# Where the expert values of a two-layer kernel are put down: by slot or by token

## The chip, the cores and the metric

The kernel runs on one core of a Trainium2 chip. The metric is the device time of one launch in microseconds (us), lower is better. The core has five instruction streams that run side by side and meet at semaphores: PE (matrix multiplication, with PEld for its weight loads), DVE (vector), ACT (scalar), POOL (general purpose) and SP (here only an issuer of DMAs). Plain DMAs are issued by SP; an indirect DMA, whose row addresses come from an index tile, is issued by POOL.

## The reference

Two layers work on x of shape 4 x 1024 x 256 (batch b, position, feature D). Each has an attention part and a mixture of experts. The mixture of layer 0, which the change is about:

```python
logits = einsum('bsd,de->bse', h, Wr) + br            # 8 experts
route_w = softmax(logits); topk 2; renormalised       # two experts per token
hid = relu(einsum('bsd,edh->ebsh', h, W1) + b1)       # 256 -> 1024
expert_out = einsum('ebsh,ehd->ebsd', hid, W2) + b2   # 1024 -> 256
x = x + gb * einsum('bse,ebsd->bsd', routed, expert_out)
```

Layer 1 first normalises this x, runs a gated product with three weights (w0, w2: 256 to 1024, w1: back) over 8 chunks of 128 positions, each chunk scaled by a decay that depends on the loss of the chunks before, and then has a second, smaller mixture (8 experts of 256 x 256, two per token). All is float32.

## The kernel before, in words

**Tokens, pairs, blocks, slots.** There are 4096 tokens in 32 tiles of 128 (tile c*4+b is chunk c of batch b). Each token has two pairs (token, expert). Only the chosen experts are computed: the pairs are sorted by expert into blocks of 128 slots, a block has one expert, and there can be up to J = 71 blocks (2*32+8-1). 68 of them are always worked through (`passed` = J - SPARE); the last 3 only in a branch that is taken if the data need them.

**Prologue** (to about 115 us). Layer 0's attention part, normalisation and router. The normalised rows go to the DRAM tensor `h_rows` (`store`, L1231), one row per token and one row of ones for empty slots. `route` (L376) marks each token's two experts; `close_staged` (L544) lays out the blocks; `limits` and `list_weights` (L675) give the tables from which the later steps work.

**Blocks** (to about 640 us). For each block j: `reach`, `look`, `find` compute which 128 tokens it holds (three blocks ahead); `fetch` gathers their rows of `h_rows` into one of four buffers `xgbuf` (two blocks ahead); `turn_rows` and `rows_turned` transpose them on PE and copy them to `xT`; `weights_in` and `weights_out` gather W1 and W2 of its expert into one of two buffers each, where a table entry out of bounds makes the gather skip weights that are there already; `hidden` (PE, p_h) and `rectified` (ACT) give the hidden rows; `values` (PE, p_y) and `biased` (DVE) the 128 values; `kept` (L1625) stores them to rows j*128 and following of the DRAM tensor `y0`. The first 60 blocks (`turning` = J - LATE) are a loop written out by hand, in which p_y runs one block behind p_h. The order in it on POOL is `weights_in(j + 1)`, `weights_out(j)`, `fetch(j + 2)`. Small steps of the side work (`once`, L1650) are strewn into it: ranks of pairs within their expert (`ranks`, `places`), routing weights, and from them `slot`, the row of `y0` at which each pair's values lie (`weights`, L751, a generator of which one step runs per block).

**The last blocks and the combination.** Blocks 60 to 67 (`late_block`, `late_values`) are pieces of a planner, `Plan`: each piece has an engine, an estimated duration, predecessors, buffers that it holds and a rank; the planner simulates the engines and writes the instructions out in the order in which it started the pieces, and that order is then fixed on each engine. Among these pieces is the combination of the first two chunks: layout and block order are such that the first 8 tiles (FIRST) have all their pairs in the first 60 blocks. `combine` (L1408) does a tile: two gathers from `y0` by `slot` into a buffer `yg` of 128 x 2 x 256 (three buffers), ACT scales the first by its routing weight, DVE adds the second, multiplies by the gate and adds to x.

**Layer 1.** A second plan holds everything after: the combination of the other six chunks, then for every chunk normalisation (`normal`), the gated product (`fast`: p_u, p_f) and layer 1's mixture, whose pairs are in two groups `ga` and `gb`, with their own gathers from `ga_y` and `gb_y`.

Every gather goes through one helper, L330, so in the profile the tiles tell them apart: `w<-in_W,g_wrow`, `xg<-h_rows,g_row`, `yg<-y,g_slot`.

Of the kernel before, what the change touches and what calls it, by code (L numbers as in the profile page):

```python
# [19 lines left out]
P = 128  # L20
# [3 lines left out]
E = 8  # L24
# [9 lines left out]
AHEAD = 3  # L34
W1ROW = KD * H + KH
# [102 lines left out]
def adaln_d2_kernel(  # L138
# [95 lines left out]
    xgbuf = [pw.tile([P, D], F32, name=f"xg_{i}") for i in range(4)]  # L234
# [34 lines left out]
    lane = iota("lane", [[0, 1]], [P, 1], mult=1)  # L269
    count = iota("count", [[1, P]], [P, P])  # L270
# [71 lines left out]
    class Pairs:  # L342
# [4 lines left out]
        def __init__(self, pool, scratch, name, n):  # L347
            def t(shape, dt, what, of=pool):
                return of.tile(shape, dt, name=f"{name}_{what}", bufs=1)

            self.n, self.J, self.name = n, blocks_of(n), name

            self.part = min(n, P // E)
            self.halves = n // self.part
            self.K = self.part * E
            self.one = t([P, 2, n, E], F16, "one")
            self.best = t([P, 2, n], F32, "best")
            self.w = t([P, 2, n], F32, "w")
            self.pos = t([P, 2, n], F32, "pos")
            self.slot = t([P, 2, n], I32, "slot")  # L360
            self.row = t([P, self.J], I32, "row")
            self.wrow = t([P, self.J], I32, "wrow")
            self.start = t([P, E], F32, "start")


            self.more = t([P, self.halves, P + 1], F16, "more")
            nc.vector.memset(self.more[:, :, P : P + 1], 1.0)
            self.limit = t([P, self.halves, self.J], F32, "limit")
            self.nth = t([P, self.J], F32, "nth")

            self.both = t([P, n + 1, E], F16, "both")
            nc.vector.memset(self.both[:, 0, :], 0.0)
            self.pairs = t([P, self.halves, P], F16, "pairs")
            self.base = t([P, self.halves], F32, "base", scratch)

        def route(self, scratch, logits, bias, at, k, step=1):  # L376
# [14 lines left out]
            for i in range(2):  # L391
# [10 lines left out]
                first = scratch.tile([P, k], F32, tag=f"r{k}_first", name="r_first", bufs=2)  # L402
# [272 lines left out]
        def list_weights(self, scratch):  # L675
# [18 lines left out]
            )  # L694

# [54 lines left out]

        def weights(self, scratch):  # L751

            n, up1, origin = self.n, self.up1, self.origin

            def t(shape, what, dt=F32):
                return scratch.tile(shape, dt, tag=f"g_{what}", name=f"g_{what}", bufs=1)


            d = t([P, n], "d")
            nc.vector.tensor_tensor(d, self.best[:, 0, :], self.best[:, 1, :], ALU.subtract)  # L760
            nc.scalar.activation(d, d, AF.Tanh, scale=0.5)
            for i, sign in ((0, 0.5), (1, -0.5)):
                nc.vector.tensor_scalar(self.w[:, i, :], d, sign, 0.5, ALU.mult, ALU.add)
            start = t([P, E], "start1")
            nc.vector.memset(start[:, E - 1 :], 0.0)
            nc.vector.tensor_copy(start[:, : E - 1], origin[:, 1:E])
            own = t([P, E], "own_n")
            nc.vector.tensor_tensor(own, up1[:, 1:], up1[:, :E], ALU.subtract)
            jump = t([P, E], "jump")
            nc.vector.tensor_tensor(jump, origin[:, E:], start, ALU.subtract)  # L770
            one = self.one.rearrange("p i n e -> p (i n) e")
            of = []
            for what, by in (("at", start), ("own", own), ("jump", jump)):
                yield
                mine = t([P, 2 * n, E], "mine")
                nc.vector.tensor_tensor(
                    mine, one, by.unsqueeze(1).to_broadcast([P, 2 * n, E]), ALU.mult
                )
                yield
                r = t([P, 2 * n], f"of_{what}")  # L780
                nc.vector.tensor_reduce(r, mine, AX.X, ALU.add)
                of.append(r)
            yield
            at, own, jump = of
            pos = self.pos.rearrange("p i n -> p (i n)")

            nc.vector.scalar_tensor_tensor(own, own, float(P), pos, ALU.mult, ALU.is_lt)
            nc.vector.tensor_tensor(own, own, jump, ALU.mult)
            nc.vector.tensor_tensor(at, at, own, ALU.add)
            nc.vector.tensor_scalar(at, at, float(P), -1.0, ALU.mult, ALU.add)  # L790
            nc.vector.tensor_tensor(
                self.slot.rearrange("p i n -> p (i n)"), at, pos, ALU.add
            )
# [25 lines left out]


# [14 lines left out]
    h_rows = dram.tile([B * S + 1, D], F32, name="h_rows")  # L835
    for k in range(KD):
        nc.sync.dma_start(h_rows[B * S :, k * P : (k + 1) * P], ones[:1, :])
    sT0 = silu_of(0, c0)
# [305 lines left out]
    def second_half(b):  # L1144
# [64 lines left out]
        for gs in routed:  # L1209
# [14 lines left out]
            for g in gs:  # L1224
                of_batch["route", b, g] = d
            for g in gs:
                back, slot, key = backs[g]

                def store(g=g, key=key):
                    at = 4 * g * B * P  # L1230
                    nc.sync.dma_start(  # L1231
                        h_rows[at : at + 4 * B * P, :].rearrange(
# [135 lines left out]
    y0 = dram.tile([g0.J * P, D], F32, name="y0")  # L1368
    for j in range(g0.J - SPARE, g0.J):
        for k in range(KD):  # L1370
            nc.sync.dma_start(y0[j * P : (j + 1) * P, k * P : (k + 1) * P], ones)
# [36 lines left out]
    def combine(key, c, kind, y, g, tile_of, bias, gate, after, rank, at=0.0):  # L1408

        done = []  # L1410
        for b in range(B):
# [3 lines left out]
            for i in range(2):  # L1415

                def fetch(b=b, s=s, i=i):
                    if i == 0:
# [3 lines left out]
                got.append(  # L1422
                    plan(
                        POOL, 1.28, fetch, after=after, holds=[slot], rank=rank, at=at, lag=1.5
                    )
                )

# [196 lines left out]
    def kept(j, y):  # L1624
        return plain(nc.sync.dma_start(y0[j * P : (j + 1) * P, :], y))  # L1625
# [22 lines left out]
    steps = g0.weights(work)  # L1648

    def once(j):  # L1650

        if j == 3:
            g0.places(work, g0.ranks(ps_m))
# [4 lines left out]
        if j >= 6:  # L1658
            next(steps, None)
# [3 lines left out]
    with tc.manual_schedule(engines=ORDERED | {EngineType.SP}):  # L1663
        for j in range(2):
            g0.fetch(xgbuf[j], h_rows, j)
        xT, hid = rows_turned(turn_rows(0)), None
        for j in range(turning):

            weights_in(j + 1)
            if j:  # L1670
                weights_out(j)
# [6 lines left out]
            xT = rows_turned(turn_rows(j + 1))  # L1678
            g0.find(work, g0.look(ps_m, reached), j + AHEAD)
            if j:  # L1680
                kept(j - 1, biased(j - 1, values(j - 1, hid)))
# [7 lines left out]
    def late_block(j):  # L1689
# [65 lines left out]
        def turned_():  # L1755
            made[key, "xT"] = rows_turned(made[key, "pt"])

        if j > turning:
            t = plan(PE, 0.27, turn, after=of_block.get(("rows", j), []), holds=[ps], rank=at - 0.6)
            d = plan(DVE, 0.45, turned_, after=[t], holds=[ps, xTs], rank=at - 0.6)  # L1760
# [19 lines left out]
    def late_values(j, hids, after):  # L1780
# [7 lines left out]
        def out_():  # L1788
            made[key, "y"] = biased(j, made[key, "p2"])

        if j == passed - 1:
# [4 lines left out]
            SP, 0.1, lambda: kept(j, made[key, "y"]), after=[d], holds=[ys], rank=at, lag=2.2  # L1796
# [3 lines left out]
    made[("b", turning - 1), "hid"] = hid  # L1800

# [26 lines left out]
    for c in range(FIRST // B):  # L1828
# [4 lines left out]
            y0[: turning * P, :],  # L1833
# [4 lines left out]
            [of_block["kept", turning - 1]],  # L1838
            50.0 + c,
        )  # L1840
# [7 lines left out]
    with tc.If(filled > passed, preferred_fallthrough_block=True, label="late"):  # L1848
# [3 lines left out]
        for j in range(passed, g0.J):  # L1852
# [6 lines left out]
            kept(j, biased(j, values(j, hid)))  # L1859
# [444 lines left out]
    for c in range(NC):  # L2304
# [3 lines left out]
        else:  # L2308
# [4 lines left out]
                y0,  # L2313
# [132 lines left out]
```

## Time and profile before

| | |
|---|---|
| time, median of 3 runs | 1153.02 us (1152.88 to 1153.03) |
| the profiled execution, its own time | 1154.62 us |
| its span, first to last instruction | 1152.6 us |
| mean granted clock of PE | 0.987 |
| busy: PE, DVE, ACT, POOL | 1100.8, 586.6, 425.1, 410.6 us |
| POOL's indirect DMAs: weights w, rows xg, values yg of layer 0 | 134, 68, 64 |
| their mean time on POOL | 998, 966, 959 ns for w, xg, yg |
| stores of y by SP | 68, of 128 KB each |

The profile is of one execution. Its busy times are sums over the span; a line such as `2.80 <-DVE xT L1572` in brackets says that the engine sat idle for 2.80 us before the instruction and that DVE's writing of `xT` at line 1572 ended it. [...] Starts and lengths of PE's matmuls are as issued; they are pipelined.

### The profile page before, as it was taken

The numbers are of one execution on the slowest core, as the hardware profiler recorded it, in microseconds if no ns is written. First come the engines' busy times: TensorE is split into PE (matmuls) and PEld (weight loads), VectorE is DVE, ScalarE is ACT, GpSimd is POOL, SyncE is SP. The second block draws the span as 40 slices with busy tenths as digits, with TensorE's granted clock in tenths as the row PEclk, the third lists the DMA queues.
The fourth block names the chain that finished last, engine by engine and source line by source line (L and its number), as shares of the span: only waits on it lengthen the run. The fifth ranks groups of instructions, "written<-read, shape, count | busy, mean of one in ns | idle before, by whom it ended". The sixth has DMA issues, their size and how long they took to land. (4 is left out here: it accounts for less than half of the span.)

```text
span 1152.6 us, 18406 instructions
## 1 busy us (share of the span) xinstructions
PE 1100.8 (96%) x6236; PEld 872.3 (76%) x6236; DVE 586.6 (51%) x2245; ACT 425.1 (37%) x1148; POOL 410.6 (36%) x477
## 2 busy tenths in 40 slices
PE   8999999999999999999989989999999999999893
PEld 5996899999999999999978455675667676646751
DVE  7777233222222212222245589878587535787566
ACT  5975333233333323233324433423324325342421
POOL 1000444333443344333463452420124332644644
PEclk8999999999999999999998999999999999999997
DMA  9412514564522415151251211200013323342544
GB/s 320 163 54 92 178 50 147 192 220 151 188 78 75 156 33 193 37 188 38 74 197 46 66 55 52 62 29 18 1 38 104 112 71 97 102 127 86 147 108 130
DMA packets 79369, 123.18 MB, mean 107 GB/s; under 512 B 23646, under 2 KB 63076, under 8 KB 74668
## 3 DMA queue, kind: packets, MB, share of 16 engines
q0 software_dynamic: 31680, 69.61, 19.9%
q1 hardware_dynamic: 46492, 50.80, 13.3%
q10 hardware_dynamic: 1104, 1.58, 0.4%
q8 instruction: 52, 0.85, 0.3%
q14 instruction: 41, 0.34, 0.1%
HBM read 205.18 MB, written 30.58 MB: 205 GB/s over the span
## 5 line engine op out<-in xcount | busy, mean ns | idle before, releaser
L1599 ACT ACTIVATE hid<-p_h,w 128x128 f32<-128x128 f32 x544 | 155.1, 368 | 338.0 <-issue 257.1
L1587 PEld LDWEIGHTS p_h<-xT,w 128*128 128x128 f32 x2176 | 255.4, 193 | 7.8 <-DVE xT L1572 4.0
L1587 PE MATMUL p_h<-xT,w 128*128 128x128 f32 x2176 | 257.1, 277 | 3.8 <-DVE xT L1572 3.2
L1610 PE MATMUL p_y<-w,hid 128*128 128x256 f32 x1088 | 251.6, 384 | 3.2 <-issue 3.2
L1884 PE MATMUL p_u<-hT,a 128*128 128x512 f32 x512 | 230.7, 595 | 0.8 <-ACTq L1848 0.8
L330 POOL DMA_INDIRECT w<-in_W,g_wrow x134 | 133.7, 998 | 271.6 <-ACT hid L1599 129.9
L1610 PEld LDWEIGHTS p_y<-w,hid 128*128 128x128 f32 x1088 | 202.6, 191 | 29.2 <-issue 4.2
L1884 PEld LDWEIGHTS p_u<-hT,a 128*128 128x128 f32 x512 | 94.2, 190 | 97.2 <-issue 89.3
L1572 DVE COPY xT<-pm_x 128x256 f32<-128x256 f32 x68 | 28.8, 424 | 186.8 <-PE pm_x L1567 176.4
L1932 PE MATMUL p_f<-a,hf 128*128 128x256 f32 x512 | 116.8, 380 | 3.9 <-DVE ln_mv L1467 1.6
L1621 DVE TENSOR_TENSOR y<-p_y,w 128x256 f32<-128x256 f32 x68 | 28.8, 424 | 176.1 <-PE p_y L1610 176.1
L1932 PEld LDWEIGHTS p_f<-a,hf 128*128 128x128 f32 x512 | 95.9, 190 | 22.6 <-issue 5.7
L330 POOL DMA_INDIRECT xg<-h_rows,g_row x68 | 65.7, 966 | 123.7 <-DVE g_hits L734 103.3
L330 POOL DMA_INDIRECT yg<-y,g_slot x64 | 61.4, 959 | 86.7 <-DVE x_sb L1444 33.5
L2193 PE MATMUL p_e<-ew,xT 128*128 x280 | 70.4, 384 | 0.3 <-ACT y L2203 0.3
L330 POOL DMA_INDIRECT xg<-ga_rows,ga_row x39 | 37.2, 954 | 91.3 <-DVE ga_row L743 35.0
L1896 ACT ACTIVATE hf<-p_u,decay 128x512 f32<-128x512 f32 x56 | 38.0, 683 | 72.6 <-PE p_u L1884 68.5
L2193 PEld LDWEIGHTS p_e<-ew,xT 128*128 128x128 f32 x280 | 49.4, 190 | 10.6 <-issue 5.1
L1507 DVE TENSOR_TENSOR h<-h,mod 128x256 f32<-128x256 f32 x128 | 51.5, 425 | 9.2 <-ACT h L1497 6.3
L1900 DVE SCALAR_TENSOR_TENSOR hf<-p_u,decay,hf 128x512 f32<-128x512 f32 x56 | 41.9, 748 | 21.8 <-PE p_u L1884 14.5
L2203 ACT COPY y<-p_e 128x256 f32<-128x256 f32 x70 | 26.0, 371 | 57.1 <-PE p_e L2193 24.8
L1980 POOL TENSOR_TENSOR x_sb<-x_sb,step 128x256 f32<-128x256 f32 x32 | 23.7, 743 | 62.2 <-DVE step L1973 44.5
(363 smaller groups left out, 1283.6 us busy)
## 6 DMA issues: line engine op xcount, KB each, us to landing
y<-y SPq DMA_DIRECT2D x68, 128.0 KB
ga_y<-y SPq DMA_DIRECT2D x39, 128.0 KB
x_sb<-in_x SPq DMA_DIRECT2D x8, 512.0 KB
h_rows<-xn SPq DMA_DIRECT2D x8, 512.0 KB
gb_y<-y SPq DMA_DIRECT2D x31, 128.0 KB
out_x<-x_sb SPq DMA_DIRECT2D x7, 512.0 KB
a<-in_fw SPq DMA_DIRECT2D x6, 512.0 KB
mod<-mod_rows SPq DMA_DIRECT2D x6, 512.0 KB
```

Source lines behind the costliest of these rows:

```text
L330: return nc.gpsimd.indirect_dma_start(out=dst, out_offset=None, in_=table, in_offset=bass.IndirectOffsetOnAxis(ap=index, axis=0), bounds_c ...
L1507: nc.vector.tensor_tensor(h, h, mods1[(sc, sh)[i]][:, b, :], (ALU.mult, ALU.add)[i])
L1572: nc.vector.tensor_copy(xT, pt)
L1587: nc.tensor.matmul(p1[:, i, :], lhsT=w1[:, k * H + m * P : k * H + (m + 1) * P], rhs=xT[:, k, :], start=(k == 0), stop=(k == KD - 1),)
L1599: nc.scalar.activation(hid[:, m, :], p1[:, i, :], AF.Relu, bias=w1buf[j % 2][:, KD * H + m : KD * H + m + 1],)
L1610: nc.tensor.matmul(p2, lhsT=hid[:, m, :], rhs=w2[:, m * D : (m + 1) * D], start=(m == 0), stop=(m == KH - 1),)
L1621: nc.vector.tensor_tensor(y, p2, w2buf[j % 2][:, KH * D :], ALU.add)
L1884: nc.tensor.matmul(pu, lhsT=a[:, k, m * P : (m + 1) * P], rhs=made["n1", c, "hT"][:, k, :, :], start=(k == 0), stop=(k == KD - 1),)
L1896: nc.scalar.activation(made[key, m], made[key, m, 0], AF.Silu, scale=decays[c])
L1900: nc.vector.scalar_tensor_tensor(h, made[key, m, 1], decays[c], h, ALU.mult, ALU.mult)
L1932: nc.tensor.matmul(made[key, "p2", b], lhsT=made[key, m][:, b * P : (b + 1) * P], rhs=a1[:, m, :], start=(m == 0), stop=(m == KH - 1),)
L2193: nc.tensor.matmul(made[key, "p2"], lhsT=made[key, "xT"][:, k, :], rhs=ew_flat[:, bass.ds(made[key, "at"] + k * D, D)], start=(k == 0), st ...
```

## The change

Each gathered row now brings with it where its values belong. A row of `h_rows` has two more elements (DX = 258): the code of the token's first expert (8 minus its number) and twice the token's place (row 2*(s*128+p) for token p of tile s). Small plain DMAs (`mark`) write both, eight bytes per token, after each call of `route`; the row of the empty slots gets a number beyond the last row. After a block's rows are transposed, `aim` computes on DVE, for each of its 128 slots, twice the token's place plus 1 if the block's expert is not the token's first. `put` stores the block's values to those rows of `y0` by an indirect DMA on POOL; rows beyond the end are skipped. `y0` now has 2 rows for each of 4096 tokens, and `combine` reads a tile's 128 x 2 x 256 values by one plain load on SP, which waits for the puts that can hold its pairs (the first 60 for the first two chunks, all for the others). In the loop the put of block j - 2 stands between `weights_in(j + 1)` and `weights_out(j)` on POOL. The ranks within an expert, `places` and the computation of `slot` are gone for layer 0, and so are the fills of the three spare blocks of `y0`. Layer 1's mixture keeps its slots and gathers.

The diff, cut to its core:

```diff
+DX = D + 2
-    xgbuf = [pw.tile([P, D], F32, name=f"xg_{i}") for i in range(4)]
+    xgbuf = [pw.tile([P, DX], F32, name=f"xg_{i}") for i in range(4)]
+    twice = iota("twice", [[2 * P, NC * B]], [P, NC * B], mult=2)
...
+            self.meta = t([P, n, 2], F32, "meta")
+            nc.vector.tensor_copy(self.meta[:, :, 1], twice[:, :n])
+            self.beyond = t([P, 2], F32, "beyond")
+            nc.vector.memset(self.beyond, float(2 * n * P))
+            self.code = t([P, self.J], F32, "code")
...
-                first = scratch.tile([P, k], F32, tag=f"r{k}_first", name="r_first", bufs=2)
+                if i == 0:
+                    first = self.meta[:, cut, 0]
+                else:
+                    first = scratch.tile(
+                        [P, k], F32, tag=f"r{k}_first", name="r_first", bufs=2
+                    )
...
+            nc.vector.tensor_scalar(
+                self.code, self.pb[:, 0, :], -1.0, float(E), ALU.mult, ALU.add
+            )
...
+        def aim(self, scratch, xg, j):
+            dest = scratch.tile([P, 1], I32, tag="g_dest", name="g_dest", bufs=8)
+            nc.vector.scalar_tensor_tensor(
+                dest, xg[:, D : D + 1], self.code[:, j : j + 1],
+                xg[:, D + 1 : D + 2], ALU.not_equal, ALU.add,
+            )
+            return dest
+
+        def put(self, table, dest, y):
+            return plain(
+                nc.gpsimd.indirect_dma_start(
+                    out=table,
+                    out_offset=bass.IndirectOffsetOnAxis(ap=dest, axis=0),
+                    in_=y,
+                    in_offset=None,
+                    bounds_check=2 * self.n * P - 1,
+                    oob_is_err=False,
+                )
+            )
...
+    def put(name, *args):
+        ins = groups_of[name].put(values_of[name], *args)
+        for others in (name, f"{name} read"):
+            tc.declare_no_dep(ins, group=others, reason="other places")
+        tc.add_to_no_dep_group(name, ins)
+        puts.setdefault(name, []).append(ins)
...
-    h_rows = dram.tile([B * S + 1, D], F32, name="h_rows")
+    h_rows = dram.tile([B * S + 1, DX], F32, name="h_rows")
+    nc.sync.dma_start(h_rows[B * S :, D:], g0.beyond[:1, :])
...
+            def mark(k=k, at=at):
+                first = at - at % B
+                nc.sync.dma_start(
+                    h_rows[first * P : (first + k * B) * P, D:].rearrange(
+                        "(c b p) d -> b p c d", b=B, p=P
+                    )[at % B],
+                    g0.meta[:, at : at + (k - 1) * B + 1 : B, :],
+                )
+            plan("SP", 1.0, mark, after=[d], rank=rank)
...
-    y0 = dram.tile([g0.J * P, D], F32, name="y0")
-    for j in range(g0.J - SPARE, g0.J):
-        for k in range(KD):
-            nc.sync.dma_start(y0[j * P : (j + 1) * P, k * P : (k + 1) * P], ones)
+    y0 = dram.tile([2 * B * S, D], F32, name="y0")
...
+            def load(b=b, s=s):
+                t = made[key, c, b] = buf(kind, [P, 2, D])
+                y = values_of[g.name][2 * s * P : 2 * (s + 1) * P, :]
+                ins = plain(nc.sync.dma_start(t, y.rearrange("(p i) d -> p i d", i=2)))
+                if stage is not None:
+                    tc.declare_no_dep(
+                        ins, group=g.name, keep=puts[g.name][:stage], reason="other places"
+                    )
+                    tc.add_to_no_dep_group(f"{g.name} read", ins)
+                behind(ins, puts[g.name][:stage])
+            if y is None:
+                f = plan(SP, 0.1, load, after=after, holds=[slot], rank=rank, at=at, lag=2.7)
+                got = [f, f]
...
-        if j == 3:
-            g0.places(work, g0.ranks(ps_m))
-        if j >= 6:
-            next(steps, None)
+        if j == 6:
+            g0.weights(work)
...
             weights_in(j + 1)
+            if j > 1:
+                kept(j - 2)
             if j:
                 weights_out(j)
             g0.fetch(xgbuf[(j + 2) % 4], h_rows, j + 2)
...
             xT = rows_turned(turn_rows(j + 1))
+            aimed(j + 1)
             g0.find(work, g0.look(ps_m, reached), j + AHEAD)
             if j:
-                kept(j - 1, biased(j - 1, values(j - 1, hid)))
+                ys0[j - 1] = biased(j - 1, values(j - 1, hid))
...
         of_block["kept", j] = plan(
-            SP, 0.1, lambda: kept(j, made[key, "y"]), after=[d], holds=[ys], rank=at, lag=2.2
+            POOL, 1.0, lambda: kept(j), after=[d], holds=[ys], rank=at, lag=2.2
         )
+    of_block["kept", turning - 2] = plan(
+        POOL, 1.0, lambda: kept(turning - 2), at=0.4, rank=-2.0, lag=2.2
+    )
...
-            y0[: turning * P, :],
+            None,
...
-            [of_block["kept", turning - 1]],
+            [of_block["kept", turning - 2], of_block["kept", turning - 1]],
             50.0 + c,
+            stage=turning,
```

## The prediction

> **What bounds the kernel now.** I read the page first, then the table of busy time by stretch, then the timeline where PE falls behind. The page, busy time of the engines and PE's row of the 40 slices:
>
> ```profile
> PE 1100.8 (96%) x6236; PEld 872.3 (76%) x6236; DVE 586.6 (51%) x2245; ACT 425.1 (37%) x1148; POOL 410.6 (36%) x477
> ...
> PE   8999999999999999999989989999999999999893
> ```
>
> PE is busy in all but 1152.6 - 1100.8 = 51.8 us. By 20 us stretches, 6.3 of the idle lie before 40 us and 17.6 after 1120; from 140 to 580 there is none. What this change can win is where its reads are: from 575 us, when the first pairs are gathered. The same table, cut at the start of the matmuls p_h of blocks 60 to 67 (the last row ends at layer 1's first p_u); columns: stretch, length, then busy us of PE, PEld, DVE, ACT, POOL, clock, DMA share, GB/s:
>
> ```profile
> 569.19:576.60 7.41, 7.41 (x55) 6.91 (x53) 1.60 (x7) 2.28 (x8) 3.23 (x4) 1.00 0.54 178
> 576.60:586.98 10.38, 7.58 (x55) 6.89 (x53) 3.58 (x12) 3.30 (x10) 6.46 (x7) 1.00 0.86 297
> 586.98:596.08 9.10, 9.10 (x53) 8.60 (x53) 4.80 (x15) 2.79 (x9) 5.81 (x6) 0.81 0.45 135
> 596.08:609.42 13.34, 10.09 (x55) 8.04 (x53) 5.99 (x25) 4.16 (x13) 6.70 (x8) 0.81 0.31 102
> 609.42:617.80 8.38, 8.32 (x52) 7.55 (x51) 5.13 (x16) 2.92 (x10) 5.01 (x6) 0.89 0.31 81
> 617.80:625.15 7.35, 7.35 (x51) 6.94 (x51) 4.83 (x14) 3.35 (x13) 3.93 (x4) 1.00 0.13 38
> 625.15:640.17 15.02, 13.04 (x81) 11.31 (x79) 8.20 (x29) 6.83 (x17) 1.00 (x1) 1.00 0.12 37
> ```
>
> A block takes 7.41 us with the two count matmuls, 7.35 without. Four blocks take 10.38, 9.10, 13.34 and 8.38, part of it at half clock. Why, shows in the timeline (bracket: idle before, and who ended it):
>
> ```profile
> 575.02 0.96 POOL L330 DMA_INDIRECT yg<-y,g_slot  x1 [2.79 <-issue]
> ...
> 580.23 0.38 PE L1567 MATMUL pm_x<-ident,xg 128*128 128x128 f32 x2
> ...
> 583.94 0.94 POOL L330 DMA_INDIRECT yg<-y,g_slot  x1 [0.30 <-issue]
> ...
> 586.50 0.42 DVE L1572 COPY xT<-pm_x 128x256 f32<-128x256 f32 x1 [5.10 <-remote]
> 586.98 5.24 PE L1587 MATMUL p_h<-xT,w 128*128 128x128 f32 x30 [2.80 <-DVE xT L1572]
> ```
>
> PE's transposes pm_x ran at 580.23, yet DVE's copy of them starts at 586.50 and PE then waits for it. The trace's semaphore updates from PE stop at 579.28 and resume at 585.76, seven within 1.0 us. The same happens in each of POOL's long runs of indirect DMAs 0.30 us apart: 8 of them in 575.02 to 584.89, 10 in 591.30 to 603.78, 6 in 608.60 to 615.95, 13 in 646.71 to 662.67, 8 in 667.63 to 677.34. PE's updates stop 3.7 to 7.5 us after the first and come back at 585.76, 605.69, 617.25, 665.20 and 677.58. In the loop, with three such DMAs per block, no silence is longer than 3.6 us; in layer 1 spacings up to 5.2 are normal, so the fifth case is weak. So I read: a long unbroken run on POOL holds back PE's signals, and whoever waits for PE stands still. All five runs hold gathers that the change takes off POOL. It is a coincidence seen five times, not yet a proof.
>
> PE waits once more while DVE works off the combination steps that came late:
>
> ```profile
> 674.42 2.42 PE L1932 MATMUL p_f<-a,hf 128*128 128x256 f32 x10 [1.59 <-DVE ln_mv L1467]
> 678.41 7.17 PE L1932 MATMUL p_f<-a,hf 128*128 128x256 f32 x32 [1.56 <-DVE step L1973]
> ```
>
> **The change, part by part.** Of the profiled execution: 1154.62 us, 1152.6 of span and 2.0 around it; it is 1.60 above the median of the runs, 1153.02.
>
> *Gathers out, loads in, blocks 62 to 67.* From 576.60 to 640.17 go 63.57 us. Undisturbed, the same PE work is three rounds with counts and two without, 3 x 7.41 + 2 x 7.35 = 36.93; the last p_h and two p_y, 10.48 (625.15 to 635.63); 16 transposes pm_t at 0.87 per eight, 1.74; the branch, 0.77. Sum 49.92, so 13.65 are lost now. POOL loses 16 gathers there (1.25 each, 20.0 us) and gets nine puts (11.3). DVE's 32.5 busy us (rows above) still fit into 50, and eight loads through three buffers are early enough for the second chunk, whose last gather starts only at 623.48 now: a tile's turn is about 1.9 to land, 0.51 on ACT and 1.3 on DVE, 3.7 in all, so eight need some 10 us. Bounds: 13.65 won; or 1.26 lost, a put ahead of w2, if the hold has another cause. I take 11.0, near the upper end, because all five runs go; 2.6 I leave for waits on loads.
>
> *664.31 to 685.42.* PE is busy 17.96 of 21.11: 3.15 lost. The gathers that feed DVE late are gone; bounds 0 and 3.15, taken 2.6. From 685 to 840 PE has no idle: the other gathers give 0.
>
> *Slots of pairs.* The five pm_rank matmuls make their round 7.74 instead of 7.41 (p_y at 142.84, next at 150.58): -0.3. The DVE steps (eight of 0.68, some smaller) lie where DVE is busy 27 to 33%: 0.
>
> *One put per block on POOL.* Price by the row of the fetch, 0.96, and the usual 0.30. The loop's round on POOL:
>
> ```profile
> 303.25 0.99 POOL L330 DMA_INDIRECT w<-in_W,g_wrow  x1 [2.14 <-DVE g_reached L708]
> 304.55 0.96 POOL L330 DMA_INDIRECT xg<-h_rows,g_row  x1 [0.30 <-issue]
> 307.53 0.99 POOL L330 DMA_INDIRECT w<-in_W,g_wrow  x1 [2.03 <-ACT hid L1599]
> ```
>
> The put stands ahead of w2 and xg, and waits for the y that w2 waits for already, so it delays them by 1.26 and no more; of the 2.03 free before w1, 0.77 stay, so w1 keeps its place. Xg is fetched two blocks ahead. W2 matters when the expert changes: the tightest two loads end at 215.5 and 267.7 for matmuls at 217.3 and 269.2, 1.8 and 1.5 spare, of which 0.4 go to the signal. Shifted by 1.26, and about 0.35 for 128 KB more ahead (an estimate: 128 KB at the 368 GB/s of 596 to 598), they may be 0.2 and 0.5 late. Cost 0 to 1.0; taken 0.3. Aim is one DVE step of 0.16 (row of g_row) in DVE's idle time: 0; without that cover 68 x 0.16 = 11 us.
>
> *Before the loop.* Five marks go on SP's queue among the stores of h_rows. The last route ends at 106.45; the last store of 512 KB was issued at 105.17 and landed at 108.08, 2.9 us. A mark of the same length ends at 109.4; the first fetch is at 115.28, so even one of 8.8 us is hidden. Three small DVE steps more, at most 0.23 each, one of them on the way to the first block. Cost 0 to 1.0; taken 0.2. [...]
>
> *Last put to first load.* Now y ends at 638.92 and the first gather starts 4.8 us later. A put and its landing (0.96 + 1.9, as from the gather at 575.02 to ACT's use at 577.88) are shorter than that, and PE first needs these tiles' sums in the pm_t of 694.39. Cost 0.
>
> *The planner* gets other pieces, so layer 1's order moves; PE's idle from 840 to 900, 3.2 us, is my measure: -3 to +3, taken 0.
>
> Sum: -11.0 - 2.6 - 0.3 + 0.3 + 0.2 = -13.4. Against 1154.62 that is 1141.2, and by the median 1153.02 - 13.4 = 1139.6.
>
> **Rivals.** *The hold comes from the weights, not from the gathers.* For it: the first held stretch has a DMA share of 0.86. Against: the run of 13 at 646.71 has no weights, and the longest silence, 11.0 us. Then the tail keeps about two thirds of its loss and the rest is won: 4.5 + 1 + 0.3 - 0.5 = 5.3 less, 1147.7, between 1145 and 1151. Chance 0.15.
>
> *A run of four per block holds PE's signals in the loop.* Put, w2, xg and w1 then follow with pauses of 0.30, 0.30 and 0.77. The xT copy for the next block must be done 7.42 after p_h began; pm_x signals at 3.8. If the silence begins at the third DMA (3.4 after p_h began) and ends 0.9 to 2.5 after the fourth (6.2), signals return at 7.1 to 8.7 and PE is up to 1.7 late. At 0.5 us in each of 58 blocks it costs 29, less 13.4: 1168.6. It decides from 0.25 us per block on. Against: the five silences began at about the fourth DMA of a run or later. Chance 0.11; with a bad order of layer 1, slower has 0.18.
>
> *The stall is replaced*: PE waits for loads or for w1 of block 63 in the same place; 1152. Chance 0.07.
>
> **How the numbers follow.** Faster by over 0.2% (2.3 us, about what a measurement here can tell): 0.60 for the forecast and 0.15 for the first rival; within 0.2%: 0.07; slower: 0.18. The forecast's own range is 1135.5 (all of 13.65 + 3.15 + 0.3 with nothing paid is 1135.9, and a little from the order) to 1146 (half of the tail). The range must also hold the first rival and the replaced stall, to 1152; slower and a lucky order stay outside, about 0.2.
>
> **What would show it.** Right: blocks 62 to 66 at 7.3 to 8 us each, no 0.5 clock near 590 and 605, no PE wait near 675, POOL never more than four in a row before 850, first p_u near 629, rounds of 7.41 in the loop. Wrong: rounds above 7.5 in the loop, silences of PE with only puts, w and xg on POOL, or PE waiting for yg's loads in the tail.

## The result and the profile after

The changed kernel takes 1145.44 us in the median of 4 runs (1144.39 to 1146.41), the kernel before 1153.03 (4 runs): a ratio of 0.9933, 95% interval 0.9916 to 0.9951, so 7.6 us faster. The profiled execution took 1146.41 us with a span of 1144.4; against the 1152.6 of before that is 8.2 less. How much the change is worth is not the same on every occasion: beside two later profiles of the unaltered kernel the ratio was 0.9985 (0.9974 to 0.9997) and 0.9932 (0.9915 to 0.9948). Why is the main thing that the experiments showed.

The page of after, PE's busy time and its row of the 40 slices:

```profile
PE 1096.9 (96%) x6231; PEld 870.8 (76%) x6231; DVE 590.8 (52%) x2305; ACT 425.5 (37%) x1148; POOL 422.0 (37%) x483
...
PE   8999999999999999999999999999999999899893
```

The two 8s at 580 and 600 us are gone. The table of busy time by stretch, cut at the same places as before (the rows begin with the p_h of blocks 61 to 67, there too, and the last ends at the first p_u; columns as there):

```profile
570.46:577.53 7.07, 7.07 (x51) 6.66 (x49) 2.39 (x13) 2.28 (x8) 4.98 (x5) 1.00 0.57 195
577.53:585.12 7.59, 7.53 (x54) 6.87 (x52) 4.88 (x14) 1.85 (x5) 2.17 (x2) 1.00 0.95 325
585.12:594.09 8.97, 7.86 (x52) 6.94 (x53) 6.95 (x29) 5.56 (x19) 5.06 (x5) 1.00 0.70 263
594.09:601.56 7.47, 7.47 (x53) 6.96 (x53) 6.96 (x22) 4.40 (x13) 3.98 (x4) 1.00 0.40 144
601.56:608.85 7.29, 7.29 (x53) 6.88 (x51) 6.78 (x24) 2.79 (x9) 4.29 (x5) 1.00 0.23 59
608.85:616.10 7.25, 7.25 (x52) 6.83 (x50) 5.68 (x21) 4.12 (x12) 2.02 (x2) 1.00 0.09 23
616.10:629.37 13.27, 12.42 (x82) 11.26 (x80) 1.27 (x3) 4.33 (x12) 4.09 (x4) 1.00 0.07 24
```

The four blocks that took 10.38, 9.10, 13.34 and 8.38 us take 7.59, 8.97, 7.47 and 7.29, at full clock. In the second row the DMA share is 0.95, higher than in any row of before, and PE loses 0.06 us there: the loads were not what cost. In the third row PE loses 1.11. Of this 0.81 is a wait for xT, but PE's update for the transposes was there at 589.18: DVE's copy stood behind the steps of a combination and a normalisation (588.98 to 593.62), before which DVE had idled 1.26 us (1.93 in the later profile told of below, for ACT's scaled values). Later, where PE in before waited 1.59 and 1.56 us at 674 and 678, its timeline shows no bracket any more between 636 and 838 us:

```profile
629.37 5.42 PE L1967 MATMUL p_u<-hT,a 128*128 128x512 f32 x12 [0.85 <-ACTq L1930]
635.65 19.15 PE L1967 MATMUL p_u<-hT,a 128*128 128x512 f32 x44 [0.87 <-ACT hf L1979]
```

The round of the loop on POOL, by its timeline, with the put ahead of w2 and xg; from w1 (the first row) to the next round's first DMA it is 3.13 us, as it was in before (307.53 to 310.66):

```profile
300.64 1.00 POOL L332 DMA_INDIRECT w<-in_W,g_wrow  x1 [0.67 <-ACT hid L1670]
303.77 1.02 POOL L784 DMA_INDIRECT y<-y,g_dest  x1 [2.14 <-DVE g_reached L724]
305.10 1.01 POOL L332 DMA_INDIRECT w<-in_W,g_wrow  x1 [0.31 <-PE p_h L1658]
306.41 0.98 POOL L332 DMA_INDIRECT xg<-h_rows,g_row  x1 [0.30 <-issue]
```

The whole execution by stretches between starts of PE's groups (us); pm_l of a chunk is layer 1's router matmul. The right half is a second pair of profiles, of the two unaltered kernels on one chip in one series:

| from, to | before | after | difference | before again | after again |
|---|---|---|---|---|---|
| start, first p_h | 119.45 | 120.31 | +0.86 | 118.75 | 118.06 |
| first p_h, p_h of block 60 | 442.59 | 442.24 | -0.35 | 442.59 | 442.25 |
| p_h of block 60, first p_u | 78.13 | 66.82 | -11.31 | 76.53 | 66.97 |
| first p_u, pm_l of chunk 3 | 201.40 | 198.50 | -2.90 | 204.99 | 198.07 |
| chunk 3, chunk 5 | 137.72 | 138.03 | +0.31 | 137.83 | 137.93 |
| chunk 5, chunk 6 | 47.55 | 51.14 | +3.59 | 48.31 | 50.93 |
| chunk 6, chunk 7 | 64.75 | 65.38 | +0.63 | 63.95 | 64.98 |
| chunk 7, end | 61.0 | 62.0 | +1.0 | 64.6 | 63.1 |

So about 14 us were won by 828 us, as foreseen, and 5 given back in layer 1's mixtures, most of it between chunks 5 and 6. There POOL stands still before one gather, PE runs out of work 6 us later, and half clock follows from 1001.38 to 1004.79. POOL's timeline, then a row of PE's:

```profile
986.91 0.95 POOL L332 DMA_INDIRECT yg<-ga_y,ga_slot  x1 [0.30 <-issue]
987.97 0.73 POOL L2063 TENSOR_TENSOR x_sb<-x_sb,step 128x256 f32<-128x256 f32 x1
991.25 1.00 POOL L332 DMA_INDIRECT yg<-ga_y,ga_slot  x1 [2.56 <-DVE yg L1513]
```

```profile
1000.41 0.39 PE L2080 MATMUL pm_loss<-loss,ones 128*128 128x4 f32 x2 [3.29 <-ACT diff L2050]
```

The name in POOL's bracket is only the last event before it: in four more profiles of kernels with the same gathers the stand is 2.56 us too, behind other steps of DVE. What the gather waits for the profiles do not show.

### The profile page after: what moved, and what is told of

The parts are those of the page before. It is cut to its first block, busy times and chain, and to the rows that moved or that the text cites. A ratio compares the mean times of both kernels' runs of the same rounds, so it can differ in the third digit from the quotient of the medians.

```text
span 1144.4 us, 18476 instructions
## 1 busy us (share of the span) xinstructions
PE 1096.9 (96%) x6231; PEld 870.8 (76%) x6231; DVE 590.8 (52%) x2305; ACT 425.5 (37%) x1148; POOL 422.0 (37%) x483
## 4 chain that ended last, share of the span: by engine, by line
PE 82%; DVE 7%; DMA 4%; issue 3%; ACT 2%; POOL 1%; ACTq 0%; POOLq 0%; SPq 0%; DVEq 0%
PE p_h L1658 20%; PE p_y L1681 19%; PE p_u L1967 17%; PE p_f L2015 8%; PE p_e L2276 4%; PE p_e L2324 2%; PE pm_x L2259 1%; PE pm_l L2107 1%; DMA w<-in_W,g_wrow 1%; PE pm_x L1638 1%; PE pm_counts L737 1%; PE pm_gram L1100 1%; PE pm_t L1620 1%; PE pm_b L1041 1%; PE pm_l L1233 1%
## 5 line engine op out<-in xcount | busy, mean ns | idle before, releaser
L1658 PE MATMUL p_h<-xT,w 128*128 128x128 f32 x2176 | 254.4, 275 | 1.8 <-DVE xT L1643 1.2
L1681 PE MATMUL p_y<-w,hid 128*128 128x256 f32 x1088 | 249.0, 382 | 0.3 <-issue 0.3
L784 POOL DMA_INDIRECT y<-y,g_dest x68 | 69.5, 1022 | 143.7 <-DVE g_reached L724 108.4
```

The costliest lines, as they stand in the source:

```text
L784: nc.gpsimd.indirect_dma_start(out=table, out_offset=bass.IndirectOffsetOnAxis(ap=dest, axis=0), in_=y, in_offset=None, bounds_check=2 * s ...
L1658: nc.tensor.matmul(p1[:, i, :], lhsT=w1[:, k * H + m * P : k * H + (m + 1) * P], rhs=xT[:, k, :], start=(k == 0), stop=(k == KD - 1),)
L1681: nc.tensor.matmul(p2, lhsT=hid[:, m, :], rhs=w2[:, m * D : (m + 1) * D], start=(m == 0), stop=(m == KH - 1),)
```

## The experiments

A "silence" is a stretch between two semaphore updates of PE in the trace. In layer 1 they come up to 5.2 us apart without any run on POOL. A silence alone is not yet a hold, since a trace can lack updates: that of the changed kernel has 1217 of PE, a later one of the same program 1319. So in before PE is silent from 722.00 to 730.64, 8.63 us, but nobody waited for it: DVE read PE's p_f at 723.75 and 727.28, straight after the matmuls. A hold shows where updates come later than their matmuls, in a bunch (from 585.76 in before, eight for the eight that were due), or where a waiting engine starts late. Each experiment was timed beside the kernel before, on the same chip.

**The first chunks' reads as gathers again.** The puts stay, the planner's pieces for these 8 tiles are two POOL gathers each, as before the change:

```diff
+    nc.gpsimd.iota(g0.slot, pattern=[[1, 2], [2 * P, NC * B]], base=0, channel_multiplier=2)
...
+                ins = plain(
+                    gather(made[key, c, b][:, i, :], values_of[g.name][:2 * FIRST * P, :], g.slot[:, i, s : s + 1])
+                )
...
+            if y is None and stage is not None:
+                got = [plan(POOL, 1.28, ..., lag=1.5) for i in range(2)]
```

> The changed kernel with the reads of the first two chunks of layer 1 (8 tiles, in the tail of the block loop) put back to two POOL gathers each, from the values stored by token; the puts stay, and the other six chunks keep their plain loads. If long runs of indirect DMAs on POOL hold back PE's signals (my theory): runs of six or more are back in the tail, PE's updates fall silent there, the stretch from p_h of block 62 to the first p_u of layer 1 goes from 51.8 us back to 60 to 66, and the time from 1145.4 to 1154 to 1160. If the hold came from the weights' transfers (rival): the stretch stays within 51 to 54 and the time within 1144 to 1148.

1160.92 us, ratio 1.0063 (1.0042 to 1.0084): the whole gain of the change is lost and more. From p_h of block 62 to the first p_u it is 71.3 us (51.8 without). POOL has runs of 8, 6, 6, 5 and 9 between 575 and 631, silences of 5.8 and 5.1 us end 0.3 and 1.1 us behind two of them, and PE waits in the same blocks as in before, or near them:

```profile
587.44 6.38 PE L1686 MATMUL p_h<-xT,w 128*128 128x128 f32 x32 [4.21 <-issue]
...
615.42 5.47 PE L1686 MATMUL p_h<-xT,w 128*128 128x128 f32 x32 [3.10 <-DVE xT L1671]
...
640.30 0.30 PE L1648 MATMUL pm_t<-ident,h 128*128 128x128 f32 x1 [4.38 <-DVE h L1606]
```

The weights are the same as in the changed kernel, so they are not the cause. It costs more than in before, perhaps since the puts share POOL with the gathers; this was not tried by itself.

**The other six chunks' reads as gathers again.** The same edit for `stage is None`.

> The changed kernel with the reads of the last six chunks of layer 1 (24 tiles) put back to two POOL gathers each, from the values stored by token; the first two chunks keep their plain loads. Theory: the run of gathers behind the last block holds PE's signals, and the waits of PE between 650 and 680 are back: 2 to 5 us, 1147.5 to 1150.5. Rival (gathers cost nothing here, PE has other work): within 1 us of 1145.4. What is given back in the mixtures of layer 1, near 990 us, should stay in either case if it is made there.

1144.29 us, ratio 0.9917 (0.9893 to 0.9941): not slower than the changed kernel's 0.9933, a miss. The stretches say why. From the first p_u to pm_l of chunk 3 it is 200.68 us instead of 198.50, with waits of 0.48 and 1.49 us near 661 and 665: the run of 14 gathers does cost 2.2. But between chunks 5 and 6 it is 46.59 instead of 51.14: with 48 more DMAs ahead of it, POOL's stand is not in the mixture any more. My last sentence, that what is given back would stay, was wrong, and this was the first sign of what it is.

**Runs of gathers alone.** In layer 1, where POOL has little else, 4, 8 and 16 gathers that nobody uses:

```diff
+RUNS = {(2, 0): 4, (2, 3): 8, (3, 0): 16}
...
+                if (c, m) in RUNS:
+                    go = tiny([P, 1], "go")
+                    nc.gpsimd.tensor_copy(go, h[:, :1])
+                    for i in range(RUNS[c, m]):
+                        gather(late.tile([P, D], F32, tag="probe", name="probe", bufs=6), y0, g0.slot[:, i % 2, i // 2 : i // 2 + 1])
```

> The changed kernel with runs of indirect gathers that nobody uses, put on POOL where layer 1 has nothing else there (chunks 2 and 3, about 713 to 800 us): 4, 8 and 16 in a row, each run released by a DVE step, no weights on the queue. Theory: the run of 4 holds nothing; with 8, PE's semaphore updates are silent for about 6 us, with 16 for 12 us or more, and PE, which has three buffers of 1.74 us ahead, stands 1 to 4 us in the first and 7 to 11 in the second: the time goes up by 8 to 15 us to 1153 to 1160. Rival (runs on POOL hold nothing; it was the weights, or the waits of the combination for its data): no silence above 5.2 us, PE without idle, within 1 us of 1145.4.

1155.55 us, ratio 1.0018 (1.0004 to 1.0031), 10 us above the changed kernel. The run of 4 (from 722.2) leaves no silence above 3.5 us; that of 8 (732.5 to 742.3) one of 7.5 that ends at 742.5; that of 16 (768.3 to 788.4) two of 7.6 and 5.0. PE, by its timeline, has work in hand through the run of 8 and stands 7.3 us in and after that of 16; half clock follows for 10.2 us:

```profile
781.94 1.88 PE L1969 MATMUL p_u<-hT,a 128*128 128x512 f32 x4
788.26 0.69 PE L2114 MATMUL pm_l<-rw_sb,hT 128*128 128x64 f32 x2 [4.44 <-issue]
791.84 3.25 PE L2114 MATMUL pm_l<-rw_sb,hT 128*128 128x64 f32 x14 [2.89 <-ACT hT L1631]
```

What pm_l waits for are ACT's copies of the transposes pm_t. PE ran these by 782.1, yet ACT, which is idle, makes the first copy only at 787.62, near the end of the run (788.40):

```profile
781.06 1.04 PE L1622 MATMUL pm_t<-ident,h 128*128 128x128 f32 x8
...
787.62 0.58 ACT L1631 COPY hT<-pm_t 128x512 f32<-128x512 f32 x1 [7.39 <-issue]
```

There are no weights here and no one needs the gathers. A run by itself holds PE's signals, in this series.

**One more put per block.** A second put of the same values to another table, straight behind the first, in blocks 0 to 57:

```diff
+        if j < turning - 2:
+            put("g0x", dests[j], ys0[j])
```

> The changed kernel with a second put of each block's values, to a table that nobody reads, straight behind the first, in all blocks of the loop but the last two: five indirect DMAs per block in a run (put, put, w2, xg, w1), 6.3 us of 7.41 on POOL. Theory, with the hold beginning at about the fourth of a run: PE's signals come late in each round, rounds of 7.6 to 9 us, 10 to 90 us in all. Rival (POOL has room, and w1 comes half a microsecond later only): rounds stay at 7.41, and the time goes up by 0 to 2 us, paid where the expert changes.

1178.75 us, ratio 1.0203 (1.0172 to 1.0234), 33 us above the changed kernel. From the first p_h to that of block 60 it is 477.7 us instead of 442.2: 0.61 per block. POOL now runs 6 to 9 DMAs on end in each round or two, silences of 5.7 to 7.5 us are the rule, and PE's waits between 130 and 590 us, of which the changed kernel has none up to 560, are (by waited-for; total, times, longest):

```profile
PE p_h L1660 <- DVE xT L1645: 17.4, 15, 1.6
PE pm_x L1640 <- DMA xg<-h_rows,g_row: 4.6, 6, 1.5
PE p_y L1683 <- issue: 2.1, 5, 0.6
```

The largest is the copy of xT that waits for PE's signal; late rows of xg are the second. POOL has room (a run of five, from 133.63 to 139.94, takes 6.3 of the 7.41 us), and still the fifth DMA per block undoes the change four times over.

**The changed kernel again.**

> The changed kernel once more, unaltered, for a second profile of it and for its time on the chip of the runs beside it. In its first profile POOL stood still before a gather at 991.25 us with nothing that the profile shows as awaited, PE waited 3.29 us for what hangs on it, and half clock followed at 1001.38; none of the four kernels derived from it shows this. Theory (a chance event of that execution): the two router matmuls about it, 51.1 us apart there, are 46.5 to 47.6 apart here, and the median lies at 1141 to 1144.5. Rival (it belongs to this program, by where its POOL instructions fall): 51 us again, and 1145 to 1146.

Here the two kernels are within 2 us: 1135.77 against 1137.63 for the kernel before, 0.9985 (0.9974 to 0.9997). But the rival is right about the stand: 2.56 us before the 17th gather once more, 50.3 us between chunks 5 and 6. It belongs to the program. This profile and the next three, taken in the same series, lack none of PE's updates (1319 and 1324), and not one comes over 0.1 us late while the program runs. The profiles of all other series lack about 70 to 140 of them, and in all of them some come late. Whether the recording has a part in the hold no run here tells; that PE, DVE and ACT do wait there is seen in their own instructions, not in these records.

**Four forms of a burst** (16 gathers in fours with pauses, 16 of a quarter of the bytes, 16 plain transfers, 32 arithmetic steps):

> The changed kernel with four bursts of 16 things on POOL that nobody uses, in layer 1 where POOL has nothing else (first hidden matmul of chunks 1 to 4): gathers in fours with a pause of some 2.2 us of POOL arithmetic between; gathers of a quarter of the bytes, back to back; plain transfers of 128 KB from POOL's queue; 32 arithmetic steps. Theory (it is the unbroken run of indirect DMAs, not bytes and not POOL being busy): the fours leave PE's updates silent for no more than 5.2 us, the quarter gathers hold them for two stretches of 5 to 8 us as the run of 16 did, the plain transfers and the arithmetic not at all; PE stands 5 to 8 us in the second burst alone, and the time goes up by 6 to 10 us. Rival 1 (bytes): the quarter gathers hold nothing. Rival 2 (any DMA of POOL): the plain transfers hold too. Rival 3 (POOL busy): the arithmetic holds too.

1142.53 us in a single run beside the runs of the experiment above. None of the four shows a silence above 4.2 us while it runs, the 16 quarter gathers neither, by which rival 1 would be right. PE's timeline across that burst (725.4 to 745.3) has no bracket at all. Since the full-size burst was not in this kernel, this could not be told from a chip or hour in which nothing holds; see the last experiment but one.

**The last mixture spread out, and the kernel before with pauses.** In the first, `pause(2)`, two additions on POOL of some 0.75 us each, behind each pair of gathers of `gb_y`; in the second, the same behind each of the eight pairs in the tail of the kernel before:

```diff
                     gather(made[key, c, b][:, i, :], y, g.slot[:, i, s : s + 1])
+                    if i == 1 and key == "c2" and c >= 4:    # the second: key == "c1" and c < FIRST // B
+                        pause(2)
```

> The changed kernel with a pause of two arithmetic steps on POOL, some 1.5 us, behind each pair of gathers in the last mixture of layer 1 (12 pairs, from 1100 us on), where a run of 14 gathers now keeps PE's updates silent for 8.9 us and PE waits 1.5, 1.6 and 2.5 us for DVE. Theory: the silence breaks up, the waits shrink to 1 to 3 in sum, and the time goes down by 1 to 4 us against the unaltered kernel beside it. Rival (the end hangs on the gathers themselves, and later gathers mean a later end): up by 1 to 6 us.

> The kernel before, with nothing of the change, but with a pause of two arithmetic steps on POOL, some 1.5 us, behind each of the eight pairs of gathers in the tail of the block loop. Theory (the run is what costs, not that the reads are gathers): the silences in the tail grow shorter than 5 us, the stretch from p_h of block 60 to the first p_u goes from 78.1 us to between 68 and 74, and the time down by 4 to 10 us against the kernel before. Rival (the gathers, or the values they bring late, cost by their number): the stretch stays or grows by up to 8 us, the time by 0 to 8.

Both are misses. The first: 1148.33 us, 12.6 above the unaltered kernel beside it; from pm_l of chunk 7 to the end 70.6 us instead of 56.8. The gathers are on the path that sets the end, and 24 pauses of 0.75 make them later. The second: 1143.02, ratio 1.0049 (1.0031 to 1.0066), the stretch from p_h of block 60 to the first p_u 77.9. In this series of four profiles, though, runs of 14, 16 and 20 left no silence above 5 us (two of 6.1 and 5.3 in the tail of the paused kernel lie about runs of 4 and 5 and hold PE's own waits of 2.7 and 2.8 us). There was no hold by long runs to break up, so neither says whether pauses help against one. But the second shows another way to lose time in the tail. PE's two waits are for xT, and DVE copied it late because steps of the combination stand ahead of it: one waited 8.21 us for a gather to land (until 587.78), one 4.61 for ACT, which had itself waited for a gather (until 598.86). So late gathers cost there without a held signal too, and how much of the 13.65 us lost in before goes to each is not separated.

**Both kernels once more, side by side.**

> The kernel before, unaltered, for a profile of it beside one of the changed kernel from the same chip and hour. The change was worth 7.6 us in the first comparison and 1.9 in the runs beside the second profile of it, where the kernel before took 1137.6. Theory (what the runs of gathers cost differs from chip to chip or hour to hour, and with it the worth of the change): where the two differ by less than 4 us, this profile shows the stretch from p_h of block 60 to the first p_u below 74 us and fewer half-clock stretches in it; where they differ by 7 or more, 76 to 80 us as at first. Rival (the tail is always alike, 78 us, and the difference lies elsewhere, in layer 1 or at the end): 77 to 79 us in either case.

> The changed kernel, unaltered, as the measure for the three runs beside it. Theory: POOL stands 2.56 us before the 17th gather of the first mixture once more, the router matmuls are 50 to 51 us apart, the stretch from p_h of block 60 to the first p_u is 66.5 to 70 us, and the gain over the kernel before is what that kernel's tail shows above this, plus 2 to 4 us, less the 3.5 us of the stand. Rival: the gain does not follow the tail of the kernel before.

Before 1152.60, changed 1145.18, ratio to the kernel before 0.9932. The right half of the table above is this pair: the tail 76.53 against 66.97, the stretch behind it 204.99 against 198.07 (the profiled execution of before is the longest of its 11, with a span of 1157.6 us). Runs of 8, 10, 7 and 13 in before hold again (silences of 5.8, 5.8, 6.8 and 4.8 us), with half clock at 586.7, 607.2 and 637.9. The hour in which the change was worth 1.9 us is the hour without a hold. What the tail of before was in that hour no profile shows; the theory of the first of these expectations is tested on one side only.

**Sixteen memsets ahead of the stand.**

```diff
+                if (c, m) == (2, 0):
+                    for i in range(16):
+                        nc.gpsimd.memset(tiny([P, 1], "filler", 1), 0.0)
```

> The changed kernel with 16 one-column memsets more on POOL at about 720 us, where it has nothing else. POOL's stand of 2.56 us before the 17th gather of layer 1's first mixture is the same in all three profiles that share the changed kernel's POOL instructions up to there, and in none of the five that have 16 or more others ahead. Theory (it hangs on the place of that instruction in POOL's program): no stand there, PE does not wait 2.5 to 3.3 us near 1000, the two router matmuls are 46.5 us apart instead of 50 to 51, and the time is 3 to 4.5 us below the unaltered kernel beside it. Rival (it hangs on something else): the stand stays, within 1 us.

1146.00 us, ratio 0.9929 (0.9908 to 0.9949); 2.56 us again, 52.2 between chunks 5 and 6. A miss: it isn't the place among POOL's instructions. What the profiles do have in common is the number of indirect DMAs: POOL stands before its 220th in the loop (2.56 to 2.59 us in all changed kernels whose loop is unaltered; before the 114th it is 2.16, where 0.30 is usual) and before its 326th, 106 later; in the kernel before, its two profiles and the paused one alike, before the 114th (3.6), 220th (2.1) and 325th (2.5). With 16 to 64 indirect DMAs more ahead, the 326th is another instruction and the mixture has no stand. In the kernel with quarter-size bursts (below) the 326th lies in a burst and shows nothing, so a bare count is not the whole rule.

**Full and quarter rows in turn,** four bursts of 16, back to back:

```diff
+RUNS = {(1, 0): 1, (2, 0): 4, (3, 0): 1, (4, 0): 4}
```

> The changed kernel with four bursts of 16 back-to-back gathers on POOL that nobody uses, in the first hidden matmul of layer 1's chunks 1 to 4: rows of 1 KB, of 256 B, of 1 KB, of 256 B. In earlier profiles 1 KB rows held PE's updates for 7.6 and 5.0 us and 256 B rows did not, but on different days. Theory (the bytes in flight matter, or with them the DMA engines): silences above 5.2 us in bursts 1 and 3, none in 2 and 4, 8 to 20 us more in all. Rival 1 (the instruction itself holds, whatever its bytes): silences in all four, 20 to 35 us more. Rival 2 (it is the chip or the hour): none in any, 0 to 3 us more.

1187.44 us, ratio 1.0298 (1.0276 to 1.0320), 42 above the changed kernel. All four hold: silences of 5.7, 6.3, 7.2 and 9.2 us at the longest, the two with 256 B rows no less than the others. In the second burst (quarter rows, 732.2 to 752.2), PE's timeline:

```profile
745.33 1.88 PE L1969 MATMUL p_u<-hT,a 128*128 128x512 f32 x4
755.66 3.74 PE L2120 MATMUL pm_l<-rw_sb,hT 128*128 128x64 f32 x16 [8.45 <-ACT hT L1631]
```

The same burst at the earlier series:

```profile
738.45 1.88 PE L1976 MATMUL p_u<-hT,a 128*128 128x512 f32 x4
740.17 1.89 PE L2132 MATMUL pm_l<-rw_sb,hT 128*128 128x64 f32 x16
```

So rival 1 on bytes: a gather of 256 B rows holds like one of 1 KB rows, and whether any run holds at all changes from one series to the next. The chip alone does not decide it: the record names chip 1 for the series of the first four experiments, where runs held, and for the next, 17 minutes later, where none did. The plain transfers and the arithmetic were tried only where nothing held, so for them it is open.

## Why the prediction was right, and where it was not

The likeliest case came true, with the time 5.8 us above the number (1145.4 for 1139.6). Part of this is luck: the prediction did not know that the hold comes and goes, and on the occasion where the change was worth 1.9 us its case "within 0.2%", to which it gave 0.07, would have come true. Point by point:

- **The mechanism.** That long unbroken runs of indirect DMAs on POOL hold back PE's signals was a coincidence seen five times. That they do is shown now, for the series in which anything held: runs that do nothing else do it (8 and 16, with silences of 7.5 and 7.6 us), one of 4 leaves no silence above 3.5 us, and putting 16 gathers back brings the lost time back (51.8 us become 71.3), with the same weights. Why they do is not shown. Of the five, the first three are holds by the updates that came late (8, 4 and 4). Of the six due in the fourth silence, 3 came late, the others the trace lacks, and of the three due in the fifth 1 came late. That 5.2 us was the longest usual spacing in layer 1 was a wrong reading, too: there is the 8.63 at 722.00.
- **The tail**: -11.0 taken; from p_h of block 62 to the first p_u 63.57 became 51.84, -11.73. (The rows of the prediction's table begin with block 61, not 60; its sum counts them rightly.)
- **664 to 685**: -2.6 taken, -2.90 measured, though the fifth silence was called weak; 2.2 of it came back with the gathers.
- **The loop**: -0.3 for the ranks and +0.3 for late w2 taken; -0.35 measured. No w2 is late. The put is free, but not without trace: between 125 and 555 us 92 of PE's updates come 0.1 to 1.4 us late in this profile, none in before. PE waits for none of them.
- **Before the loop**: +0.2 taken, +0.86 in this profile. The profiles of the changed kernel and of those made from it begin the loop at 117.9 to 120.3 us, so this is scatter. The 1 KB packets of the stores of `h_rows` from 80 us on took 70 ns each in the mean with rows of 1032 bytes, 48 before, and 46 for 48 in the median; why the mean alone is up, no run here shows. The marks' 4096 packets of 8 bytes took 8 ns each, and nothing waited for them.
- **The planner's order of layer 1**: 0 (-3 to +3) taken; +5.5 between chunk 3 and the end. This is the term that was mis-sized, and its reason was wrong as well. The order did not move: in the two programs POOL's last 143 instructions, from the gathers of `ga_rows` on, stand in the same order, and PE's last 1326 do too. Of the 5.5, 3.6 are POOL's stand and the half clock behind it. The change has 396 indirect DMAs instead of 392 and other ones ahead, so the stand falls before the 17th gather of the mixture instead of the 20th, where PE waited only 0.41 us for it. What the prediction lacked is a count of POOL's indirect DMAs, for which before showed the rows: an idle of 2.50 us with "issue" as its releaser at 1010.63. The rest (1.9) is within what the two pairs of profiles scatter at the end (61.0 to 64.6).
- **The signs.** No half clock near 590 and 605, no wait near 675, the first p_u at 629.37: as foretold. Wrong were "never more than four in a row" on POOL, which has five from 563.2 and from 571.2, with no silence above 4 us, and "7.3 to 8 us" for block 63, which took 8.97 because of the order on DVE told above.
- **The rivals.** The weights fell to the gathers put back and to the runs alone. The run of four per block does hold, by up to 1.4 us as said, but PE has that much in hand; with five it has not, at 0.61 us per block. It was nearer than 0.11 suggests. The replaced stall did not come.

The clock's share was missing from the sum as a term of its own. Every wait of PE that is followed by a half-clock stretch in these profiles costs twice: after 2.06 us (at 593.6 in the second profile of the changed kernel) 3.4 us at half clock, with 8.45 us 13.7, of which 6.0 lie within the wait; waits of 0.81, 1.35, 1.44 and 1.79 in the same place were followed by none, nor was one of 2.47 at 1127.94 in before. Up to the last mixture the stretches are multiples of 3.41 us (3.41 and 6.83 in before, 10.24 and 3.41 in after). The length of the wait alone does not decide: 2.06 us was enough in one case, and 2.47 not in another.

## What to carry to other kernels

Look at POOL's indirect DMAs as a sequence, not by their busy time: where six or more followed each other 0.3 us apart, an engine that waited for PE got its signal late in some series, near the end of the run (in before DVE's copy at 586.50, for transposes that ran at 580.23, with a run to 584.89), and PE's clock fell behind that (0.81 in the blocks from 586.98 to 609.42). Look for the waiting engine that starts late, not only for a silence in the updates, which can be a gap in the trace (1217 updates of PE in one profile, 1319 in another of the same program). And look at what stands ahead of the step that PE waits for on its engine: a combination that waited for its values held up the copy of xT with no signal late (PE waited 2.7 and 2.8 us in the paused kernel). Plain loads from a table that was written in the reader's order took such runs away here (78.13 us of tail became 66.82); one indirect DMA more per round of the loop built new ones (6 to 9 on end, 0.61 us per block). Measure such a gain on more than one occasion: here it was 7.6 us on two and 1.9 on a third.

## What the runs showed of the hardware that was not expected

- Runs of 8 and more indirect DMAs on POOL hold PE's semaphore updates (5.4 us from the first matmul's end at 580.39 to 585.76 in before), whether rows of 1 KB or 256 B are gathered (silences of 5.7 to 9.2 us in the four bursts). In one series of four profiles they held nothing: 16 in 20 us, no silence above 4 us. Runs of four held them by up to 1.4 us, in the same series as the long ones.
- In every profile with late updates the trace lacks updates as well, 5 to 11% of PE's, and in the four without it lacks none.
- POOL stands for 2.0 to 3.6 us before its 114th, its 220th and its 325th or 326th indirect DMA, in most of the profiles. Why, and what is counted, no run here settles.
- From one series to the next, with the same program, the kernel before took 1153.0, 1154.0, 1137.6 and 1152.8 us; the changed one, in the first and the last two, 1145.4, 1135.8 and 1145.2.
